# Attention steps in a fused attention and Hadamard-MLP kernel: order of bank emptying, place of the residual, and places of x transposes, values and folds

## The chip, the core and the metric

The kernel runs on one core of one Trainium2 chip. The metric is the time of the whole program on the device in microseconds (us); times given are medians of several runs, and beside them stands one profiled execution, from which all durations come. TensorE is called PE in the profile, VectorE DVE, ScalarE ACT, GpSimd POOL, SyncE SP. SP issues nearly all DMAs.

## What is computed

The input x has 8 batches of 512 rows with 512 features. One attention layer and one MLP layer follow each other, each with a layer norm ahead of it, a layer norm behind it and a residual sum:

```python
x = x + _layernorm(_L0_attn_ref(_layernorm(x, axis=-1), ...), axis=-1)
x = x + _layernorm(_L0_ffn_ref(_layernorm(x, axis=-1), ...), axis=-1)
```

The attention has 16 heads of 32 features. Its scores come from rotated queries and keys alone, since the rotary part is as wide as the head:

```python
c_kv = x @ W_dkv + b_dkv
v = (c_kv @ W_uv + b_uv).reshape(B_, S_, N_HEADS, D_HEAD)
c_q = x @ W_dq + b_dq
q_rot = apply_rotary((c_q @ W_qr + b_qr), cos, sin)
k_rot = apply_rotary((x @ W_kr + b_kr), cos, sin)
scores = einsum('bqhd,bkhd->bhqk', q, k) / sqrt(D_HEAD)
attn = softmax(scores)
out = einsum('bhqk,bkhd->bqhd', attn, v) @ W_o + b_o
```

The MLP is a gated one (512 to 2048 to 512) with Walsh-Hadamard transforms ahead of both matrix products. The second transform is folded into W_down: during the attention part, the kernel transforms W_down once, 32 of its 512 columns at a time (16 folds), and keeps the result in DRAM for the MLP.

## The kernel before

The program has two parts. The attention part runs to about 930 us, the MLP part behind it. The change lies in the attention part.

The attention of a batch is cut into 4 groups of 4 heads, and a group into 4 steps (one for each 128 keys). A batch so has 16 steps, called step 0 to step 15 here (`i` in the code; `c = i % 4` is the step in its group), and the part has 128 steps. The order of every instruction is written out by hand (`manual_schedule`); the engines work through their own queues in that order and wait for each other by semaphores.

In a step, PE gets these in turn:

- `scores_t` (lines 556 to 584): transposed scores `t` of 4 heads by 128 keys and 512 queries, in two score tiles of two banks each. Four bf16 matmuls (L564) put the negated row maximum in, eight matmul instructions (L573) add the scores. ACT takes the exponential of either tile (L584) into `p`.
- `weigh` (L602) of the step before: the product of `p` with the values, gathered in the bank `ops`. At the end of a group ACT copies it to `osb` (L611).
- in the third step of a group `sums` (L618), in the last `bias_rows`: four small transposes (L550) of the row maxima `parts`, which ACT copies to `brow` (L554) for the `t` of the next group.
- the piece of the table `BETWEEN`, unless the step is in `TWO`
- `row_max` (L527): the scores `s` of the step six ahead, whose row maxima DVE takes (two reduces, L535)
- the piece of `BETWEEN` in steps of `TWO`, this time in a score tile, and then the piece of the table `BEHIND`

Pieces are what the next batch (or the last one) needs: transposes of x (`x_flip`, L393, four transposes), the compressed queries and keys (`compress`, L406), keys and queries with their rotation (`key` L438, `query` L454, `rotate` L413), values (`value`, L466), the output projection of the batch before (`out_proj`, L656 and L657) and folds of W_down (`fold`, L485, with four levels on DVE, L493 and L494, one in each of the steps that follow, and a store by SP). With the rotation, ACT adds the bias, DVE shuffles (L419), and POOL makes two products and a sum (L420 to L422).

PSUM has three pools: `ps_s` with three score tiles of two banks, through which `t`, `s` and the pieces of `TWO` steps rotate, `ps_o` with one bank for `ops`, and `ps_f` with one bank, which all other pieces, the sums and the bias rows share. A piece can only start when the one before it has been copied out.

POOL gets the sums of neighbouring `p` (`add_up`, L590, four instructions in the second and in the fourth step of a group), the rotations, the inverse deviations (L104, L105), the residual sums (L689, in steps 10 to 13, by `early`), and the `split` of row maxima into three bf16 parts (L543 to L545, in the second step of a group). DVE has beside the reduces the sums of pairs (`add_pairs`, L595, first step of a group), statistics of rows, the division (L652) and the levels of the folds.

Of the kernel before, what the change touches and what calls it, by code (L numbers as in the profile page):

```python
# [10 lines left out]
F32 = mybir.dt.float32  # L11
# [22 lines left out]
def sandwich_kernel(  # L34
# [218 lines left out]
    with ExitStack() as actx:  # L253
# [127 lines left out]
        def x_norm(b, t):  # L381
            rs, sh = stats[b]
            xn[b, t] = row.tile([P, D], F32, tag="xn", name=f"xn_{b}_{t}", bufs=3)
            nc.scalar.activation(
                xn[b, t], xs[b][:, t, :], AF.Identity, bias=sh[:, t : t + 1], scale=rs[:, t : t + 1]
            )
# [130 lines left out]
        def row_max(n, qc):  # L517

            b, g = divmod(n, NK)
            if qc == 0:  # L520
                nms[n] = sm.tile([P, NT, GH], F32, tag="nm", name=f"nm_{n}")
            sp = [
                ps_s.tile([P, 2, S], F32, tag="s", name=f"s_{n}_{qc}_{h}") for h in range(2)
            ]
            for j in range(GH):
                rows = slice(j * DH, (j + 1) * DH)
                nc.tensor.matmul(  # L527
                    sp[j // 2][:, j % 2, :],
                    lhsT=qT[b][rows, g, ts(qc, P)],
                    rhs=kT[b][rows, g, :],  # L530
                    start=True,
                    stop=True,
                )
            for h in range(2):
                nc.vector.tensor_reduce(  # L535
                    nms[n][:, qc, 2 * h : 2 * h + 2], sp[h], AX.X, ALU.max, negate=True
                )
# [18 lines left out]
        def scores_t(n, c):  # L556

            b, g = divmod(n, NK)
            sp = [
                ps_s.tile([P, 2, S], F32, tag="s", name=f"t_{n}_{c}_{h}") for h in range(2)  # L560
            ]
            for j in range(GH):
                rows = slice(j * DH, (j + 1) * DH)
                nc.tensor.matmul(  # L564
                    sp[j // 2][:, j % 2, :],
                    lhsT=ones_b[rows, :],
                    rhs=brow[n][rows].rearrange("p t q -> p (t q)"),
                    start=True,
                    stop=False,
                )  # L570
            for j in range(GH):
                rows = slice(j * DH, (j + 1) * DH)
                nc.tensor.matmul(  # L573
                    sp[j // 2][:, j % 2, :],
                    lhsT=kT[b][rows, g, ts(c, P)],
                    rhs=qT[b][rows, g, :],
                    start=False,
                    stop=True,
                )
            for h in range(2):  # L580
                pt[n, c, h] = pp.tile(
                    [P, 2, S], F32, tag=f"p{c % 2}{h}", name=f"p_{n}_{c}_{h}", bufs=3 - c % 2
                )
                nc.scalar.activation(pt[n, c, h], sp[h], AF.Exp)  # L584

        def add_up(n, c):

# [9 lines left out]
        def weigh(n, c):  # L597
            b, g = divmod(n, NK)
            if c == 0:
                o_ps[n] = ps_o.tile([P, S], F32, tag="o", name=f"ops_{n}")  # L600
            for j in range(GH):
                nc.tensor.matmul(  # L602
                    o_ps[n][j * DH : (j + 1) * DH, :],
                    lhsT=vv[b][:, c, ds(g * P + j * DH, DH)],
                    rhs=pt[n, c, j // 2][:, j % 2, :],
                    start=(c == 0),
                    stop=(c == NT - 1),
                )
            if c == NT - 1:
                o_sb[n] = op.tile([P, S], F32, tag="osb", name=f"osb_{n}")  # L610
                nc.scalar.copy(o_sb[n], o_ps[n])  # L611

        def sums(n, parts=(2,)):

# [132 lines left out]
        row_max(0, 0)  # L747
        value(0, 0)
        row_max(0, 1)
        row_max(0, 2)  # L750
        key(0, 2)
        row_max(0, 3)
        query(0, 2)
        split(0)
        turn()
        for t in range(2):
            x_norm(1, t)
        x_flip(1, 0)
        row_max(1, 0)
# [3 lines left out]


        BETWEEN = {
            0: (x_flip, 1, 1), 1: (value, 0, 2), 4: (x_flip, 1, 2),
            8: (query, 1, 0), 9: (query, 1, 1), 12: (query, 1, 2),
        }
        BEHIND = {
            0: (value, 0, 1), 1: (key, 0, 3), 2: (query, 0, 3), 3: (value, 0, 3),  # L770
            4: (x_flip, 1, 3), 5: (compress, 1, "cq"), 6: (key, 1, 0), 7: (out_proj, -1, 0),
            8: (out_proj, -1, 1), 9: (out_proj, -1, 2), 10: (out_proj, -1, 3),
            11: (key, 1, 1), 12: (compress, 1, "ckv"), 13: (value, 1, 0), 14: (key, 1, 2),
            15: (x_flip, 2, 0),
        }
        OUT = {7: 0, 8: 1, 9: 2, 10: 3}

# [1 line left out]
        APART[NG - 2], APART[NG - 1] = (0, 2, 3), (0, 1, 2, 3)  # L779


        FOLDS = [3, 8, 13, 18, 24, 29] + [
            NK * NT * b + i for b in range(2, NB - 1) for i in (5, 13)
        ]
        READ = [0] + [g - 3 for g in FOLDS[1:]]

        TWO = (1, 5, 8, 9, 12)

        def piece(table, b, i, wide=False):
            if b == 0 and table is BEHIND and i == 8:  # L790
                out_bias()
            if i in table:
                fn, d, what = table[i]
                if 0 <= b + d < NB:
                    fn(b + d, what, *([True] if wide else []))
            if table is BETWEEN and NK * NT * b + i in FOLDS:
                fold(FOLDS.index(NK * NT * b + i), wide)
            if b == NB - 1 and (i, table is BEHIND) in ENTRY:
                in_step(*ENTRY[i, table is BEHIND], 2 * NT)
# [18 lines left out]
        def early(b, i):  # L818

            if b > 0 and i - 3 in OUT:  # L820
                residual(b - 1, OUT[i - 3])
            if b + 2 < NB:
                if i >= 14:
                    x_norm(b + 2, i - 14)
            if i < 2 and 0 < b + 1 < NB:
                x_norm(b + 1, i + 2)

        def later(b, i):

# [14 lines left out]
        for t in range(NG * NT):  # L844
            n, c = divmod(t, NT)
            b, i = divmod(t, NK * NT)
            if b == NB - 1 and i == NK * NT - AHEAD + 1:
                end.append(True)
            scores_t(n, c)
            turn()  # L850
            if c == 0 and n > 1:
                invert(n - 2)
            if c == 3 and n > 1:
                divide(n - 2)
            last_steps = t + AHEAD >= NG * NT
            if last_steps:
                piece(BETWEEN, b, i)
            if t > 0:
                weigh(*divmod(t - 1, NT))
            if c == 1 and n < NG - 1 or c == 3 and n < NG - 2:  # L860
                add_up(n, c)
            if n > NG - NK:
                if c == 1:
                    sums(n - 1, APART[n - 1])
            elif c == 2 and n > 0:
                sums(n - 1)
            if c == NT - 1 and n + 1 < NG:
                bias_rows(n + 1)
            if not last_steps and (i not in TWO or b == NB - 1):
                piece(BETWEEN, b, i)  # L870
            early(b, i)
            u = t + AHEAD
            if u < NG * NT:
                row_max(*divmod(u, NT))
                if u % NT == NT - 1:
                    split(u // NT)
            turn()
            if c == 0 and 0 < n <= NG - NK:
                add_pairs(n - 1)
            later(b, i)  # L880
            if b == 0 and i == 6:
                out_bias_in()
            if levels:
                levels.pop(0)()
            if small:
                small.pop(0)()
            if t in READ:
                fold_load(READ.index(t))
            if b == NB - 2 and i == 12:
                for j in range(3):  # L890
                    in_load(j)
            elif b == NB - 2 and i == 13:
                in_stats(0)
                in_stats(1)
            elif b == NB - 2 and i == 14:
                in_shift(0)
                in_shift(1)
            elif b == NB - 2 and i == 15:
                in_norm(0)
            elif b == NB - 1 and 2 <= i < 5:  # L900
                load_unit(*units[i - 2])
            elif b == NB - 1 and 12 <= i:
                load_row(b, i - 12)
            elif b == NB - 1 and i == 8:
                combine(*units[0][1:])
            if i in TWO and b < NB - 1:
                piece(BETWEEN, b, i, True)
            piece(BEHIND, b, i)
            if n == NG - 1 and c == 2:
                invert(NG - 2)  # L910

        weigh(NG - 1, NT - 1)
        b = NB - 1
        last = [
            ps_s.tile([P, 2, S], F32, tag="s", name=f"ps_y_{b}_{h}") for h in range(2)
# [560 lines left out]
```

## Time and profile before

| | us |
|---|---|
| median of 3 runs | 2175.89 (2175.66 to 2177.71) |
| the profiled execution | 2173.1 |
| its span, first to last instruction | 2171.3 |
| first `t` of batch 0 | 50.8 |
| first `t` of batches 1 to 7 | 155.5, 270.7, 382.1, 493.5, 604.9, 716.3, 826.5 |

The profile's page has the busy time of each engine, the chain that ended last and the costliest groups of instructions. A query for a stretch gives the same for that stretch: its busy columns stand in the order PE, PEld (weight loads), DVE, ACT, POOL, each with its count of instructions, then the granted clock of PE, the share of DMA and GB/s. The view of waits has a line for each waiting engine and line: who was waited for, us in total, times, longest. The timeline has start and length in us, engine, line, operation and tile (output<-input), and in brackets how long the engine stood idle ahead of it and who ended that. Busy times of PE include short waits, since the ends of matmuls are modelled.

### The profile page before, as it was taken

The page shows a single profiled execution, that of the slowest core. Times are in us where ns is not written, and L with a number is a line of the kernel's source. Part 1 is how long each engine was busy: PE and PEld are TensorE (multiplying, and loading weights), DVE is VectorE, ACT ScalarE, POOL GpSimd, SP SyncE. Part 2 cuts the span into 40 slices and gives each one's busy share as a digit, 9 for nine tenths or more (in the row PEclk, how much of TensorE's full clock was granted, in tenths as well). Part 3 has the DMA queues.
Part 4 walks back from the last instruction along what each step waited for, and adds up shares of the span by engine and source line. Part 5 has one row for each costly group of instructions (what it writes and reads, how often), then busy time and mean ns, then how long its engine had stood idle before and what let it go on. Part 6 is the DMA issues. An engine that isn't in the chain of part 4 may idle for free.

```text
span 2171.3 us, 24623 instructions
## 1 busy us (share of the span) xinstructions
PE 2115.1 (97%) x8552; PEld 971.1 (45%) x8552; DVE 1360.4 (63%) x2111; ACT 701.9 (32%) x1050; POOL 1352.1 (62%) x1433
## 2 busy tenths in 40 slices
PE   7999999999999999999999999999999999999998
PEld 3323333333333332334444465655556565555553
DVE  6686768686868676465655755657555557455432
ACT  3444555545454545522221121121122211111211
POOL 4686878787878879754554266464565644444542
PEclk9999999999999999999999999999999999999999
DMA  3112112111211122244344334242342333333321
GB/s 118 40 21 55 49 40 59 40 50 50 50 50 49 31 61 68 74 154 150 125 163 130 113 112 145 97 143 95 105 152 78 136 107 114 138 119 119 136 66 68
DMA packets 172252, 199.22 MB, mean 92 GB/s; under 512 B 85712, under 2 KB 114512, under 8 KB 172128
## 3 DMA queue, kind: packets, MB, share of 16 engines
q1 hardware_dynamic: 171776, 196.57, 28.7%
q8 instruction: 67, 1.10, 0.2%
q0 software_dynamic: 352, 1.08, 0.1%
q14 instruction: 57, 0.47, 0.1%
HBM read 154.24 MB, written 43.11 MB: 91 GB/s over the span
## 4 chain that ended last, share of the span: by engine, by line
PE 74%; DVE 10%; POOL 9%; issue 3%; DMA 2%; ACT 2%; POOLq 0%; SPq 0%; DVEq 0%; ACTq 0%
PE psy L1217 17%; PE d L1071 12%; PE g L1050 10%; PE u L1050 9%; POOL p L590 4%; PE s L527 3%; DVE nm L535 3%; PE ps_y L657 3%; PE t L573 3%; PE ops L602 3%; PE psz L1379 3%; PE ps_k L438 2%; PE ps_cq L406 1%; PE t L564 1%; DVE p L595 1%
## 5 line engine op out<-in xcount | busy, mean ns | idle before, releaser
L1217 PE MATMUL psy<-wd,g 128*128 128x512 f32 x896 | 436.9, 594 | 1.5 <-DVE g L1142 1.5
L535 DVE TENSOR_REDUCE nm<-s 128x2 f32<-128x1024 f32 x256 | 300.8, 1217 | 205.8 <-PE s L527 205.7
L590 POOL TENSOR_TENSOR p<-p,p 128x512 f32<-128x512 f32 x244 | 325.5, 1365 | 27.1 <-PE ops L602 19.4
L584 ACT ACTIVATE p<-t 128x1024 f32<-128x1024 f32 x256 | 248.2, 1021 | 104.1 <-PE t L573 104.1
L1091 POOL TENSOR_TENSOR h<-du,dm 128x256 f32<-128x256 f32 x92 | 66.8, 726 | 251.0 <-DVE du L1090 237.7
L1217 PEld LDWEIGHTS psy<-wd,g 128*128 128x128 f32 x896 | 169.8, 190 | 99.0 <-issue 82.5
L527 PE MATMUL s<-kT,qT 32*128 32x512 f32 x1024 | 156.7, 639 | 1.6 <-DVE nm L535 1.6
L1050 PE MATMUL u<-T,w_u 128*128 128x512 f32 x328 | 151.5, 592 | 2.8 <-DVE u3g L1169 2.8
L1050 PE MATMUL g<-T,w_g 128*128 128x512 f32 x328 | 151.3, 592 | 0.7 <-DVE T L248 0.7
L573 PE MATMUL t<-qT,kT 32*128 32x512 f32 x1024 | 142.9, 597 | 0.0
L602 PE MATMUL ops<-p,v 128*32 128x512 f32 x1024 | 136.8, 605 | 0.0
L1084 ACT COPY dm<-d 128x256 f32<-128x256 f32 x92 | 33.7, 366 | 299.0 <-PE d L1071 298.9
L438 PE MATMUL ps_k<-xT,wkr_sb 128*128 128x512 f32 x256 | 117.5, 601 | 0.8
L657 PE MATMUL ps_y<-wo_sb,oT 128*128 128x512 f32 x256 | 115.8, 593 | 0.6 <-DVE oT L652 0.6
L1050 PEld LDWEIGHTS g<-T,w_g 128*128 128x128 f32 x328 | 62.2, 190 | 78.6 <-issue 75.1
L1050 PEld LDWEIGHTS u<-T,w_u 128*128 128x128 f32 x328 | 61.8, 190 | 78.7 <-issue 73.2
L1071 PE MATMUL d<-tt,w 128*128 128x256 f32 x368 | 94.6, 380 | 0.4 <-DMA w<-w2d 0.3
L1050 PE MATMUL g<-xb,w_g 128*128 128x512 f32 x200 | 92.6, 592 | 1.2 <-issue 1.2
L1050 PE MATMUL u<-xb,w_u 128*128 128x512 f32 x200 | 92.5, 592 | 0.0
L1090 DVE TENSOR_TENSOR du<-d,du 128x256 f32<-128x256 f32 x92 | 39.1, 425 | 80.1 <-PE d L1071 76.6
L1071 PEld LDWEIGHTS d<-tt,w 128*128 128x128 f32 x368 | 69.6, 190 | 39.3 <-issue 27.0
L527 PEld LDWEIGHTS s<-kT,qT 32*128 32x128 f32 x1024 | 48.4, 183 | 78.0 <-issue 48.6
(242 smaller groups left out, 3781.0 us busy)
## 6 DMA issues: line engine op xcount, KB each, us to landing
wd<-wdd SPq DMA_DIRECT2D x112, 256.0 KB, 2.7
w_g<-wsd_g SPq DMA_DIRECT2D x24, 896.0 KB, 4.5
w_u<-wsd_u SPq DMA_DIRECT2D x23, 896.0 KB, 4.7
w<-w2d SPq DMA_DIRECT2D x23, 768.0 KB, 6.1
xr<-in_x SPq DMA_DIRECT2D x32, 256.0 KB, 2.9
xin<-x1d SPq DMA_DIRECT2D x32, 256.0 KB, 2.7
xres<-x1d SPq DMA_DIRECT2D x32, 256.0 KB, 3.2
out<-fy SPq DMA_DIRECT2D x32, 256.0 KB, 2.0
```

The costliest lines, as they stand in the source:

```text
L438: nc.tensor.matmul(ps, lhsT=wkr_sb[:, k, ts(g, P)], rhs=xT[b][:, k, :], start=(k == 0), stop=(k == NK - 1),)
L527: nc.tensor.matmul(sp[j // 2][:, j % 2, :], lhsT=qT[b][rows, g, ts(qc, P)], rhs=kT[b][rows, g, :], start=True, stop=True,)
L535: nc.vector.tensor_reduce(nms[n][:, qc, 2 * h : 2 * h + 2], sp[h], AX.X, ALU.max, negate=True)
L573: nc.tensor.matmul(sp[j // 2][:, j % 2, :], lhsT=kT[b][rows, g, ts(c, P)], rhs=qT[b][rows, g, :], start=False, stop=True,)
L584: nc.scalar.activation(pt[n, c, h], sp[h], AF.Exp)
L590: nc.gpsimd.tensor_add(into, into, pt[n, c, j // 2][:, j % 2, :])
L602: nc.tensor.matmul(o_ps[n][j * DH : (j + 1) * DH, :], lhsT=vv[b][:, c, ds(g * P + j * DH, DH)], rhs=pt[n, c, j // 2][:, j % 2, :], start=( ...
L657: nc.tensor.matmul(ps, lhsT=oT[b][:, k, ts(qc, P)], rhs=wo_sb[:, k, :], start=False, stop=(k == NK - 1),)
L1050: nc.tensor.matmul(ps, lhsT=w[:, SLOT[n], k, :], rhs=rhs[:, k, :], start=k == 0, stop=k == 1)
L1071: nc.tensor.matmul(ps, lhsT=lhs[m], rhs=rhs[m], start=True, stop=True)
L1091: nc.gpsimd.tensor_add(up[:, HS:], u3, m5)
L1217: nc.tensor.matmul(ys_[t], lhsT=g[:, ts(t, P)], rhs=w, start=n == 0, stop=n == NI - 1)
```

## The change

Six things are altered, and no operation is added or removed.

- The exponential of the second score tile: in the last step of a group it is issued behind `bias_rows`, and so behind the copy of `brow` on ACT. In the other steps it stays where it was.
- The copy of `ops` to `osb` gets a function of its own, `weighed`, which is called behind the piece of `BETWEEN`.
- `early` (the residual, the norm of x) is called behind `row_max` and `split`, no more ahead of them.
- Pieces change their steps: in `BETWEEN`, x transposes stand in steps 0, 1, 4 and 13; in `BEHIND`, values stand in steps 0, 3, 13 and 15, and steps 4 and 15 lose their x transposes. Value 1 of batch 0 is made ahead of the first step. The norms of x are issued in steps 12, 14, 15 and 0 in place of 14, 15, 0 and 1.
- Folds stand in steps 4 and 10 of batches 2 to 6 (before: 5 and 13), and at 4, 9, 14, 20, 26 and 31 of the first two batches (before: 3, 8, 13, 18, 24 and 29). In a step of `TWO` they take a score tile, in others they stand behind the piece of `BEHIND` and take the bank of the pieces.
- `TWO` is (8, 9, 10, 12, 14, 15), before (1, 5, 8, 9, 12).

```diff
--- before.py
+++ after.py
@@ -577,11 +577,15 @@
                     start=False,
                     stop=True,
                 )
-            for h in range(2):
+
+            def weight(h):
                 pt[n, c, h] = pp.tile(
                     [P, 2, S], F32, tag=f"p{c % 2}{h}", name=f"p_{n}_{c}_{h}", bufs=3 - c % 2
                 )
                 nc.scalar.activation(pt[n, c, h], sp[h], AF.Exp)
+
+            weight(0)
+            return lambda: weight(1)
 
         def add_up(n, c):
 
@@ -606,9 +610,10 @@
                     start=(c == 0),
                     stop=(c == NT - 1),
                 )
-            if c == NT - 1:
-                o_sb[n] = op.tile([P, S], F32, tag="osb", name=f"osb_{n}")
-                nc.scalar.copy(o_sb[n], o_ps[n])
+
+        def weighed(n):
+            o_sb[n] = op.tile([P, S], F32, tag="osb", name=f"osb_{n}")
+            nc.scalar.copy(o_sb[n], o_ps[n])
 
         def sums(n, parts=(2,)):
 
@@ -747,13 +752,14 @@
         row_max(0, 0)
         value(0, 0)
         row_max(0, 1)
+        value(0, 1)
         row_max(0, 2)
         key(0, 2)
         row_max(0, 3)
         query(0, 2)
         split(0)
         turn()
-        for t in range(2):
+        for t in range(3):
             x_norm(1, t)
         x_flip(1, 0)
         row_max(1, 0)
@@ -763,15 +769,15 @@
 
 
         BETWEEN = {
-            0: (x_flip, 1, 1), 1: (value, 0, 2), 4: (x_flip, 1, 2),
-            8: (query, 1, 0), 9: (query, 1, 1), 12: (query, 1, 2),
+            0: (x_flip, 1, 1), 1: (x_flip, 1, 2), 4: (x_flip, 1, 3),
+            8: (query, 1, 0), 9: (query, 1, 1), 12: (query, 1, 2), 13: (x_flip, 2, 0),
         }
         BEHIND = {
-            0: (value, 0, 1), 1: (key, 0, 3), 2: (query, 0, 3), 3: (value, 0, 3),
-            4: (x_flip, 1, 3), 5: (compress, 1, "cq"), 6: (key, 1, 0), 7: (out_proj, -1, 0),
+            0: (value, 0, 2), 1: (key, 0, 3), 2: (query, 0, 3), 3: (value, 0, 3),
+            5: (compress, 1, "cq"), 6: (key, 1, 0), 7: (out_proj, -1, 0),
             8: (out_proj, -1, 1), 9: (out_proj, -1, 2), 10: (out_proj, -1, 3),
             11: (key, 1, 1), 12: (compress, 1, "ckv"), 13: (value, 1, 0), 14: (key, 1, 2),
-            15: (x_flip, 2, 0),
+            15: (value, 1, 1),
         }
         OUT = {7: 0, 8: 1, 9: 2, 10: 3}
 
@@ -779,12 +785,13 @@
         APART[NG - 2], APART[NG - 1] = (0, 2, 3), (0, 1, 2, 3)
 
 
-        FOLDS = [3, 8, 13, 18, 24, 29] + [
-            NK * NT * b + i for b in range(2, NB - 1) for i in (5, 13)
+        FOLDS = [4, 9, 14, 20, 26, 31] + [
+            NK * NT * b + i for b in range(2, NB - 1) for i in (4, 10)
         ]
         READ = [0] + [g - 3 for g in FOLDS[1:]]
 
-        TWO = (1, 5, 8, 9, 12)
+
+        TWO = (8, 9, 10, 12, 14, 15)
 
         def piece(table, b, i, wide=False):
             if b == 0 and table is BEHIND and i == 8:
@@ -793,7 +800,7 @@
                 fn, d, what = table[i]
                 if 0 <= b + d < NB:
                     fn(b + d, what, *([True] if wide else []))
-            if table is BETWEEN and NK * NT * b + i in FOLDS:
+            if NK * NT * b + i in FOLDS and (table is BETWEEN) == (i in TWO):
                 fold(FOLDS.index(NK * NT * b + i), wide)
             if b == NB - 1 and (i, table is BEHIND) in ENTRY:
                 in_step(*ENTRY[i, table is BEHIND], 2 * NT)
@@ -819,11 +826,10 @@
 
             if b > 0 and i - 3 in OUT:
                 residual(b - 1, OUT[i - 3])
-            if b + 2 < NB:
-                if i >= 14:
-                    x_norm(b + 2, i - 14)
-            if i < 2 and 0 < b + 1 < NB:
-                x_norm(b + 1, i + 2)
+            if b + 2 < NB and i in (12, 14, 15):
+                x_norm(b + 2, max(i - 13, 0))
+            if i == 0 and 0 < b + 1 < NB:
+                x_norm(b + 1, 3)
 
         def later(b, i):
 
@@ -846,7 +852,10 @@
             b, i = divmod(t, NK * NT)
             if b == NB - 1 and i == NK * NT - AHEAD + 1:
                 end.append(True)
-            scores_t(n, c)
+            second = scores_t(n, c)
+            ends_group = c == NT - 1 and n + 1 < NG
+            if not ends_group:
+                second()
             turn()
             if c == 0 and n > 1:
                 invert(n - 2)
@@ -857,6 +866,9 @@
                 piece(BETWEEN, b, i)
             if t > 0:
                 weigh(*divmod(t - 1, NT))
+            if ends_group:
+                bias_rows(n + 1)
+                second()
             if c == 1 and n < NG - 1 or c == 3 and n < NG - 2:
                 add_up(n, c)
             if n > NG - NK:
@@ -864,23 +876,23 @@
                     sums(n - 1, APART[n - 1])
             elif c == 2 and n > 0:
                 sums(n - 1)
-            if c == NT - 1 and n + 1 < NG:
-                bias_rows(n + 1)
             if not last_steps and (i not in TWO or b == NB - 1):
                 piece(BETWEEN, b, i)
-            early(b, i)
+            if c == 0 and n > 0:
+                weighed(n - 1)
             u = t + AHEAD
             if u < NG * NT:
                 row_max(*divmod(u, NT))
                 if u % NT == NT - 1:
                     split(u // NT)
+            early(b, i)
             turn()
             if c == 0 and 0 < n <= NG - NK:
                 add_pairs(n - 1)
             later(b, i)
             if b == 0 and i == 6:
                 out_bias_in()
-            if levels:
+            if levels and i > 0:
                 levels.pop(0)()
             if small:
                 small.pop(0)()
@@ -910,6 +922,7 @@
                 invert(NG - 2)
 
         weigh(NG - 1, NT - 1)
+        weighed(NG - 1)
         b = NB - 1
         last = [
             ps_s.tile([P, 2, S], F32, tag="s", name=f"ps_y_{b}_{h}") for h in range(2)
```

## The prediction

> **What bounds the kernel now.** I read the totals of the page, then the waits of TensorE in the attention part alone, then its order of time at the places where those waits lie.
>
> ```profile
> span 2171.3 us, 24623 instructions
> PE 2115.1 (97%) x8552; PEld 971.1 (45%) x8552; DVE 1360.4 (63%) x2111; ACT 701.9 (32%) x1050; POOL 1352.1 (62%) x1433
> 493.50:604.90 111.40, 109.08 (x617) 37.58 (x616) 83.04 (x102) 57.82 (x76) 89.74 (x91) 1.00 0.19 49
> ```
>
> The third line is a busy table over one batch (steps of batch 4): TensorE 109.1 of 111.4 us, POOL 89.7, DVE 83.0. TensorE is the bound, and the diff neither adds nor removes a matmul of it. The listed waits of TensorE between 60 and 930 us add to 21 us only:
>
> ```profile
> PE t L564 <- DVE nm L535: 9.7, 16, 1.5
> PE ps_b L550 <- POOL parts L545: 4.3, 6, 0.9
> PE ps_v L466 <- ACT xT L396: 1.4, 6, 0.2
> PE ps_y L656 <- ACT brow L554: 1.2, 6, 0.2
> ```
>
> But ends of matmuls are modelled, so short waits hide in "busy". I therefore took from the timeline the time from the start of one group of matmuls to the start of the next, and subtracted the shortest such spacing of the same pair of groups in all 128 steps. Per step 0 to 15, mean of batches 2 to 5, in us: 1.10, .27, .49, .48, .48, .48, .11, .27, .18, .27, .01, .29, .29, 0, .43, .90: 6.05 a batch. Batches 0 and 1 lose 10.2 and 7.7, batch 6 5.5, batch 7 7.9. So 55 us in all can be had at most, 2.5%.
>
> Two kinds of wait make nearly all of it. First the score banks: `t` and `s` rotate through three double banks, so the second half of the next `t` needs the first row maximum of this step. The s group begins at T, its first reduce ends at T + 2.45 (493.05 + 1.2 against s at 491.87 below), TensorE needs 1.07 for s and then d for what stands behind it. The wait is 1.38 - d: .78 behind an x transpose (d = .6), .32 behind a value (1.06), .42 behind a fold (.96), none behind a 3.6 us projection. Second the one bank of the pieces, which ACT must empty. The step border 15 to 0 shows both, with POOL's queue ahead of it:
>
> ```profile
> 488.11 1.45 POOL L689 TENSOR_TENSOR y<-xr,y 128x512 f32<-128x512 f32 x1
> 491.24 0.25 POOL L545 CAST parts<-nm 128x16 bf16<-128x16 f32 x1
> 491.54 0.40 PE L550 MATMUL ps_b<-ident_b,parts 128*128 128x128 bf16 x4 [0.83 <-POOL parts L545]
> 491.87 1.14 PE L527 MATMUL s<-kT,qT 32*128 32x512 f32 x8
> 492.94 0.66 PE L393 MATMUL xt<-ident,xn 128*128 128x128 f32 x4
> 493.05 2.35 DVE L535 TENSOR_REDUCE nm<-s 128x2 f32<-128x1024 f32 x2 [1.97 <-PE s L527]
> 493.53 0.39 PE L564 MATMUL t<-brow,ones_b 32*128 32x512 bf16 x2
> 494.32 0.39 PE L564 MATMUL t<-brow,ones_b 32*128 32x512 bf16 x2 [0.41 <-DVE nm L535]
> ```
>
> The reader sees the residual's 1.45 us ahead of the split, .83 us of TensorE waiting for the split, then .79 between the halves of `t`.
>
> **What the Trainium skill says.** "PSUM — Partial Sum Buffer", Specifications: 8 banks of 512 fp32; the pools here take 6 + 1 + 1, so no bank is spare, and the waits above agree. "TensorE: Matmul & The Clock Gate", Architectural detail: ScalarE and VectorE are strict FIFO, so a late instruction delays all behind it; the trace agrees (starts keep program order). "SBUF — State Buffer", Who interferes with whom: DVE and GpSimd share a port pair as an exclusive lock; a DVE tensor_tensor with two SBUF inputs contends, tensor_reduce never. The trace agrees: half a fold level takes .42 us with POOL idle and 1.44 beside it, while a reduce stays at 1.2:
>
> ```profile
> 426.65 0.41 DVE L493 TENSOR_TENSOR fa<-fz 128x256 f32<-128x256 f32 x1
> 426.99 0.42 DVE L494 TENSOR_TENSOR fa<-fz 128x256 f32<-128x256 f32 x1
> 481.73 1.44 DVE L493 TENSOR_TENSOR fa<-fz 128x256 f32<-128x256 f32 x1
> 483.09 1.49 DVE L494 TENSOR_TENSOR fa<-fz 128x256 f32<-128x256 f32 x1
> ```
>
> **The change part by part**, for a batch of 2 to 5.
>
> *Second exponential behind brow (last step of a group).* brow's copy starts after its transposes (516.09 in step 3 of batch 4) instead of after the second exponential (516.6), so .45 earlier. The waits of `ps_y` (.27, step 7) and `ps_k` (.19, step 11) go: -.45; a 3.6 us piece follows, so no bank wait takes their place. In step 3 the value's .16 goes, but `t` then waits to .32 in all: 0. The exponential itself ends about 1 us later, 517.7, and frees its bank .4 us before the next `t`: free. If that cover went, it would cost up to .3 a group.
>
> *Residual behind the split.* Only in step 13 do both fall together. POOL's five small casts come 1.27 to 1.45 earlier: the .90 of step 15 goes. The residual's own reader, a store two steps later, isn't near.
>
> *`osb` copied behind the transposed x.* The value's .31 in step 0 goes, but its `t` then meets the bank wait .32: 0.
>
> *Pieces moved.* Step 15 gets a value for an x transpose: bank wait .79 to .32, -.47. Step 1 has a transpose ahead of s for a value in a score bank: its .25 wait for the exponential goes, one more change of tile shape costs .09. Step 2's .49 came from the wide bank and a level on DVE in steps 0 and 1; both are gone. Steps 3 to 5: the fold stands behind s in step 4 in place of a transpose, -.37. Step 13 keeps .32. x_norm (.82 on ACT) moves from steps 0, 1, 14, 15 to 12, 14, 15, 0: ACT is 52% busy, its slack in step 12 is over 1 us: 0. SP: the fold's load and store move one to six steps, each has three steps of slack; loads of x wait for x_norm one step earlier: 0.
>
> Sum so far -.45 -.90 -.47 -.25 +.09 -.49 -.37 = -2.84.
>
> *The second fold, step 13 to step 10.* Its four levels move from steps 13, 14, 15, 0 to 11, 12, 13, 14, the only part that can cost. On DVE the level of step 12 stands ahead of the shuffle of q and of the reduces of step 13. Today:
>
> ```profile
> 476.63 1.23 DVE L111 SCALAR_TENSOR_TENSOR sh_y<-mvy,rs_y 128x1 f32<-128x1 f32 x1
> 477.79 0.73 DVE L419 STREAM_SHUFFLE rot_q<-lin_q 128x512 f32<-128x512 f32 x1
> 477.80 1.27 POOL L689 TENSOR_TENSOR y<-xr,y 128x512 f32<-128x512 f32 x1
> 479.45 2.36 DVE L535 TENSOR_REDUCE nm<-s 128x2 f32<-128x1024 f32 x2 [0.93 <-PE s L527]
> ```
>
> There is .93 us of slack. I moved this queue on by hand. Step 10 is longer by .96 (fold), step 11 shorter by .19, so TensorE's `t` of step 13 stands at 475.8. The level in step 11 runs beside POOL's sums (L590, 1.22 each) and ends at 471.7; k's shuffle, rc and the reduces of step 12 end at 475.05 (today 472.8), the pair sums, alternating with POOL, at 478.5, the shift at 479.85. POOL then has nothing but q's rotation, which needs the shuffle: it is idle, so the level of step 12 takes its short .8, and the first reduce runs 481.3 to 482.5. s has been ready since 479.85. `t` of step 14 could start at 480.8 (step 13 is .4 shorter without the fold) and waits until 482.55: 1.75 in place of .32, **+1.43**. POOL ends the sums of step 13 at 490.7, the split at 492.7; its transposes are due at 493.4: no wait in step 15. Bounds: 0 if the level of step 11 finds gaps in POOL's sums; +4.3 if both levels take 2.9 (wait 3.7) and the split is late again by .9.
>
> Net -1.4 a batch, batches 2 to 6: -7.0.
>
> *Batch 1*: its step 1 loses 1.59, to a fold level on DVE: .32 after; with the same items as above, +.4 for a fold in a score bank of step 15 that waits for the delayed exponential, and +1.43: -2.3. *Batch 0*: value 1 goes among the first row maxima, where TensorE waits for DVE (16 matmuls from 32.63 to 38.29): its 1.06 is hidden, -1.06, or 0 if not; a fold fills step 9's bank wait (-.7) and the .58 of step 15 goes, while levels cost some .4: -2.0 in all. *Batch 7*: behind step 15 of batch 6 now stands a value, where nothing stood: 1.85 to .32: -1.6 with the rest.
>
> Sum -7.0 - 2.3 - 2.0 - 1.6 = **-12.9 us**. The profiled execution took 2173.1 (span 2171.3), so 2160.2; the median, 2175.9, lies 2.8 above it: **2163.0**.
>
> **Rivals.** (1) *No crowding on DVE*: the level of step 11 slips into gaps; then 1.43 x 7 = 10 us more are won, **2153**. For it: levels of .42 exist; against: POOL runs without a gap from 457 to 500. (2) *Waits are only handed on*: the split is late again because POOL is behind, and brow's .45 turns up elsewhere: 1.35 x 7 = 9.5 back, **2172**. For it: two of my items already end so. (3) *Slower*: in steps 11 to 13 DVE and POOL lock each other out twice, the reduce of step 13 comes 2 us later than I say, and the late POOL delays the split by .9: 2.9 x 7 = +20, **2183**. It decides from a wait of 3.6 us in step 14 on. For it: batch 0, which has levels in steps 11 and 12 today, shows .94 in step 14 without any of the output projection's work; against: POOL stands still while it waits for the shuffle, which shortens the level.
>
> **How the numbers follow.** Forecast .50 (own range 2157 to 2170), rival 1 .20, rival 2 .17, rival 3 .13. A measurement tells about .2% from no change, 4.4 us: 2171.5 to 2180.2 is "same". Forecast, rival 1 and a third of rival 2 are faster: .75; the rest of rival 2 same: .12; rival 3 slower: .13. Range 2152 to 2174: all but rival 3 and the tails.
>
> **What would show it.** After: no wait of ps_b for parts; xT and brow gone from TensorE's waits; step 15's half-wait of .79 down to .32; the reduce of step 13 directly behind q's shuffle and 1.2 to 1.8 us between the halves of `t` in step 14; POOL idle before q's rotation. Past 920 us nothing may move. Wrong if step 14 shows .3 or over 3 us, or if the split still ends last in step 15.

## The result, and the profile after

The changed kernel takes 2161.6 us (median of 4 runs, 2160.6 to 2162.6) against 2176.3 before (4 runs): a ratio of 0.9932, 95% interval 0.9914 to 0.9949. The profiled execution took 2160.6 us, with a span of 2158.8. So 14.7 us are won by the medians, 12.5 by the spans; the forecast was 12.9.

From the first `t` of batch 0 to the last of batch 7 the profiled executions differ by 9.9 us.

The list of the change leaves out one alteration that the diff shows: no fold level is taken in step 0 any more (`levels and i > 0`). For the folds of batches 2 to 6 it does nothing, because with their new places no level would come due there. It acts on two folds of the first two batches.

These lines are of the page and of the busy table of batch 4 of the changed kernel (columns as before).

```profile
span 2158.8 us, 24605 instructions
PE 2111.5 (98%) x8552; PEld 969.0 (45%) x8552; DVE 1348.7 (62%) x2111; ACT 703.1 (33%) x1050; POOL 1353.6 (63%) x1433
487.53:597.13 109.60, 108.81 (x618) 37.17 (x618) 79.94 (x102) 57.80 (x77) 90.17 (x91) 1.00 0.20 49
```

The batch takes 109.6 in place of 111.4 with the same matmuls. DVE's busy time fell by 3 us although it does the same: the 16 instructions of the fold levels took 13.6 us in place of 17.5, the pair sums 12.8 in place of 11.3, and the reduces of the row maxima the same to .1. The waits of TensorE in the attention part are now these, among others.

```profile
PE t L564 <- DVE nm L535: 12.2, 14, 1.9
PE ps_b L550 <- POOL parts L545: 0.9, 1, 0.9
PE ps_b L550 <- ACT p L585: 0.8, 5, 0.2
```

The waits for `parts` fell from 4.3 to 0.9 (one, in batch 0), those for `xT` and for `brow` behind a group's border are no longer there, and the wait for the row maximum has grown from 9.7 to 12.2 in fewer places. The last line is what is left in step 15 of batches 1 to 5. The border of steps 15 and 0 (batches 3 and 4), where before `t` waited .79 and `ps_b` .83:

```profile
484.42 0.59 POOL L545 CAST parts<-nm 128x16 bf16<-128x16 f32 x1
484.91 1.26 POOL L694 TENSOR_TENSOR y<-xr,y 128x512 f32<-128x512 f32 x1
485.07 0.40 PE L550 MATMUL ps_b<-ident_b,parts 128*128 128x128 bf16 x4 [0.17 <-ACT p L585]
485.40 1.14 PE L527 MATMUL s<-kT,qT 32*128 32x512 f32 x8
486.47 1.12 PE L466 MATMUL ps_v<-wuv_sb,ckv 128*128 128x512 f32 x2
487.53 0.71 PE L564 MATMUL t<-brow,ones_b 32*128 32x512 bf16 x4
487.86 0.81 PE L573 MATMUL t<-qT,kT 32*128 32x512 f32 x4
```

The residual (L694) now stands behind the last cast, the transposes follow the cast within .06 us, and the four matmuls of `t` are one row again: between 487.53 and 487.86 lies a wait of .10, and its second part (.22) comes behind the row at 487.86, .32 in all. The value behind `s` fills what the x transpose did not.

Ahead of the transposes the view names ACT's exponential, which ended at 485.04, .03 behind the last cast. It isn't what they wait for: in the kernel of the second experiment below they start .2 us before that exponential ends. So the split still ends last in step 15, and .24 us of waiting are left.

The two traces were then laid side by side by the start of each step's first `t`. Change per step, changed kernel less before, in us, batches 3 to 5 (equal to .02 in all three): step 0 -.78, 1 -.22, 2 -.49, 3 -.16, 4 +.31, 5 -1.01, 7 -.25, 10 +.95, 11 -.19, 13 -.47, 14 +.68, 15 -.19; sum -1.81. Some of these are work that changed its step (a fold from 5 to 4, from 13 to 10; .46 more work in step 15). By batch, 0 to 6: -.9, -2.5, 0, -1.8, -1.8, -1.8, -2.1; batch 7 up to its last `t` +.9. The rest is .9 ahead of the first `t` (step 0 of batch 0 is .93 longer in return, which its -.9 contains) and 1.7 behind the last `t`, in the MLP part, which took 1252 to 1255 us in the executions of all kernels here, however their attention part looked.

The crowding on DVE, ahead of step 14; the first three lines are the level of step 11 and the pair sums of step 12:

```profile
461.85 1.50 DVE L493 TENSOR_TENSOR fa<-fz 128x256 f32<-128x256 f32 x1
463.28 1.48 DVE L494 TENSOR_TENSOR fa<-fz 128x256 f32<-128x256 f32 x1
467.66 3.63 DVE L599 TENSOR_TENSOR p<-p,p 128x1024 f32<-128x1024 f32 x2
471.22 1.22 DVE L111 SCALAR_TENSOR_TENSOR sh_y<-mvy,rs_y 128x1 f32<-128x1 f32 x1
471.79 1.14 PE L527 MATMUL s<-kT,qT 32*128 32x512 f32 x8
472.36 0.41 DVE L493 TENSOR_TENSOR fz<-fa 128x256 f32<-128x256 f32 x1
472.70 0.41 DVE L494 TENSOR_TENSOR fz<-fa 128x256 f32<-128x256 f32 x1
473.05 0.72 DVE L419 STREAM_SHUFFLE rot_q<-lin_q 128x512 f32<-128x512 f32 x1
473.66 2.33 DVE L535 TENSOR_REDUCE nm<-s 128x2 f32<-128x1024 f32 x2
473.84 1.27 POOL L420 TENSOR_TENSOR lin_q<-lin_q,cs 128x512 f32<-128x512 f32 x1 [1.42 <-DVE rot_q L419]
473.92 0.39 PE L564 MATMUL t<-brow,ones_b 32*128 32x512 bf16 x2
474.92 0.39 PE L564 MATMUL t<-brow,ones_b 32*128 32x512 bf16 x2 [0.61 <-DVE nm L535]
```

`s` starts at 471.79, so its maximum could be taken from 472.97 on; DVE comes to it at 473.66, behind the level of step 12 and the shuffle, and POOL stands idle for 1.42 us meanwhile. 1.00 us lies between the halves of `t`: less the .22 that they need, and with the .22 behind it, a wait of 1.01.

### The profile page after: what moved, and what is told of

Read it like the earlier page. It is cut to its first block, busy times and chain, and to the rows that moved or that the text cites. A ratio compares the mean times of both kernels' runs of the same rounds, so it can differ in the third digit from the quotient of the medians.

```text
span 2158.8 us, 24605 instructions
## 1 busy us (share of the span) xinstructions
PE 2111.5 (98%) x8552; PEld 969.0 (45%) x8552; DVE 1348.7 (62%) x2111; ACT 703.1 (33%) x1050; POOL 1353.6 (63%) x1433
## 4 chain that ended last, share of the span: by engine, by line
PE 86%; DVE 9%; POOL 2%; issue 1%; ACT 1%; DMA 0%; SPq 0%; POOLq 0%; DVEq 0%; ACTq 0%
PE psy L1230 17%; PE d L1084 13%; PE u L1063 10%; PE g L1063 10%; PE s L527 5%; PE ps_y L662 5%; PE ops L606 5%; PE ps_k L438 4%; PE t L573 4%; PE psz L1392 3%; DVE nm L535 2%; PE t L564 2%; PE l L623 1%; DVE p L599 1%; PE ps_cq L406 1%; PE fxh L223 1%
## 5 line engine op out<-in xcount | busy, mean ns | idle before, releaser
L599 DVE TENSOR_TENSOR p<-p,p 128x1024 f32<-128x1024 f32 x56 | 86.1, 1577 | 0.0
```

The lines of the kernel that those rows point to most:

```text
L599: nc.vector.tensor_add(into, into, pt[n, 0, h])
```

## Experiments

All were measured beside the kernel before, whose median was 2177.1 to 2177.4 in them. An edit is against the changed kernel, if nothing else is said. Since runs of one kernel differ by up to 8 us, the verdicts rest on the steps of the profiled executions. In batches 3 to 6 these agree to some .02 us where nothing was changed. Single steps of the other batches don't: step 1 of batch 1 differs by 1.60 and step 6 of batch 2 by 1.65 us between kernels that are the same there.

**Is it the levels that make step 14 wait?**

```diff
-            if levels and i > 0:
+            if levels and (i > 0 or b > 2) and not (b > 1 and i in (11, 12)):
```

> The changed kernel, but the levels of the fold of step 10 (batches 2 to 6) wait until steps 13, 14, 15 and 0, where they stood before the change; the fold itself stays in step 10. Theory (VectorE's queue: the level of step 12 stands ahead of the shuffle of q and of the reduces of step 13): the wait in step 14 falls from 1.01 to 0.32 and the 0.24 of step 15 goes, 0.93 us in each of batches 2 to 5, so about 3.7 us in all: 2158. Rival A (the wait of step 14 comes from the transpose and its bank in step 13, not from the levels): no change, 2161.6, step 14 stays at 1.0. Rival B (the level in step 0 brings back step 2's wait of 0.49, as in the kernel before): 2 us of it are lost again, 2160.

Measured 2165.5 us (ratio 0.9955, 0.9941 to 0.9968), slower than the changed kernel. Step 14 fell to .32 in batches 2 to 5, and the .24 of step 15 went in batches 3 to 5, as the theory has it; rival A is out. But step 2 lost 1.9, 2.0 or 3.5 us in batches 3 to 6 (the level stands in step 0 ahead of it), not .49: rival B is right in kind and much too small in size. In the kernel before, a value and a key stood behind `s` in step 1, now only the key. That this lost cover makes the difference in size was not tested.

**The level in step 1 instead of 0**

```diff
-            if levels and i > 0:
+            if levels and i > 0 and not (b > 1 and i in (11, 12)):
```

> The changed kernel; in batches 2 to 6 the levels of the fold of step 10 wait until steps 13, 14, 15 and 1 (not 0, where the pair sums stand). Theory (what came back in step 2 with late levels was the level in step 0, behind the pair sums and ahead of the reduces of step 1): step 2 stays at 0, step 14 at 0.32 and step 15 at 0, in batches 2 to 5: -3.7 us against the changed kernel, 2158. Rival (a level anywhere in steps 0 to 2 costs it, since step 1 has only the key behind its reduces): step 2 or 3 gains 1 to 3 us of waiting, 2162 to 2170.

Measured 2158.2 us (0.9913, 0.9900 to 0.9927). Batches 3 to 5 take 108.67 us in place of 109.60: step 14 at .32, step 15 at 0, step 2 at 0, as expected. This settles the +1.43 of the forecast's queue as mechanism; its size was .69, and .24 in step 15. Step 0 of batch 7 became 2.5 us shorter as well, and step 5 of batch 7 2.7 longer.

**The three orders, undone one at a time**

```diff
+            early(b, i)
             u = t + AHEAD
...
-            early(b, i)
             turn()
```

> The changed kernel, with the residual and the norm of x ahead of row_max and split again. Theory (POOL's queue is what the bias rows of step 15 wait for; today they start 0.06 us after the parts are done): the residual's 1.27 to 1.45 us on POOL come on top in step 15 of batches 1 to 5, and about half of it in batch 6: +7 us, 2169. Rival (the gain of this edit was handed on, POOL has slack): +0 to +1.5 us, at most 2163.

Measured 2167.8 us (0.9965, 0.9951 to 0.9979). Step 15 is longer by 1.33 to 1.34 in each of batches 1 to 5, .87 in batch 6; 2.2 of it come back in step 0 of batch 7. POOL's queue is the one that the bias rows wait for.

```diff
             ends_group = c == NT - 1 and n + 1 < NG
-            if not ends_group:
-                second()
+            second()
...
             if ends_group:
                 bias_rows(n + 1)
-                second()
```

> The changed kernel, with both exponentials ahead of the copy of brow in the last step of a group. Theory: the bank waits 0.27 in step 7 and 0.19 in step 11 come back in all but the first batches, 0.45 a batch, and the value in step 15 waits as in step 3, which its next bank wait absorbs: +3 us, 2164.6. Rival (brow also gates the value of step 15 and the t of the next group by its full 0.45 to 1 us, 32 groups): +10 us or more, 2172.

Measured 2163.9 us (0.9944, 0.9930 to 0.9959). +.25 in step 7 and +.19 in step 11, in batches 1 to 6; +.16 in step 3 and -.16 in step 4: the forecast's three items to .02. But step 14 became .20 to .25 shorter in batches 1 to 4, which the forecast did not have: most likely the .19 of step 11 gives the queue on DVE that much more time. Batches 3 and 4 so lose .2 each, not .44. The rival is out.

```diff
                 weigh(*divmod(t - 1, NT))
+                if c == 0:
+                    weighed(n - 1)
...
-            if c == 0 and n > 0:
-                weighed(n - 1)
```

> The changed kernel, with the copy of ops to osb behind the product again, so ahead of the copy of the transposed x on ScalarE. Theory: the value of step 0 waits 0.31 for its bank and the t behind it waits 0.31 less for the row maximum; the same in step 4 with the fold: 0, 2161.6. Rival (the wait of the value is not absorbed): 0.31 in step 0 and in step 4 of 7 batches, +4 us, 2166.

Measured 2164.7 us (0.9950, 0.9936 to 0.9963). The last `t` is at 908.2 us against 906.7, of which .65 was there at the second step of batch 0. Steps 0 and 1: +.31 and -.31; steps 4 and 5: +.31 and -.21. The wait is handed on, but for .10 a batch. By its median this kernel is 3.0 us slower than the changed one, nearer to the rival's 2166. But of the 3.4 us between the profiled executions 2.0 lie behind the last `t` (1254.1 against 1252.1), where the edit changes nothing, and the steps speak for the theory.

**Orders alone, places alone.** The first is the kernel before with the three orders; the second the changed kernel with all three edits above.

> The kernel before, with the three orders alone (second exponential behind brow, residual behind split, osb behind the transposed x), all pieces, folds and norms in their old places. Theory (each order removes one wait of the kernel before): step 15 loses its 0.9, step 7 0.25, step 11 0.19, while the 0.31 of step 0 and the 0.16 of step 3 turn up one step later; 1.35 a batch in batches 2 to 5, about 1 in batches 0, 1 and 6 together with less in 7: -7.5 us against the kernel before, 2169. Rival (the orders only pay with the new places): -2 us at most, 2174.

Measured 2183.7 us (1.0030, 1.0021 to 1.0040): **slower than before**. Steps 15, 7 and 11 won their .88, .25 and .19, but steps 1 and 2 lost 1.7 and .6 to 2.3 in batches 3 to 6. Neither theory nor rival had that. DVE and POOL in steps 0 and 1 of batch 4, and TensorE's wait:

```profile
504.91 4.39 DVE L599 TENSOR_TENSOR p<-p,p 128x1024 f32<-128x1024 f32 x2
509.22 1.48 DVE L493 TENSOR_TENSOR fw<-fa 128x256 f32<-128x256 f32 x1
510.63 1.48 DVE L494 TENSOR_TENSOR fw<-fa 128x256 f32<-128x256 f32 x1
512.03 2.34 DVE L535 TENSOR_REDUCE nm<-s 128x2 f32<-128x1024 f32 x2
506.29 6.94 POOL L594 TENSOR_TENSOR p<-p,p 128x512 f32<-128x512 f32 x4 [0.28 <-PE ops L606]
513.29 0.39 PE L564 MATMUL t<-brow,ones_b 32*128 32x512 bf16 x2 [1.42 <-DVE nm L535]
514.43 0.39 PE L564 MATMUL t<-brow,ones_b 32*128 32x512 bf16 x2 [0.74 <-DVE nm L535]
```

In the kernel before, the same pair sum took 2.35 us, since POOL happened to stand still from 500.5 to 502.0:

```profile
500.53 2.35 DVE L595 TENSOR_TENSOR p<-p,p 128x1024 f32<-128x1024 f32 x2
502.00 6.04 POOL L590 TENSOR_TENSOR p<-p,p 128x512 f32<-128x512 f32 x4 [1.50 <-ACT p L584]
```

With step 15 shortened, step 0 begins sooner, but POOL has the residual behind the split now: its sums of the group before begin 2.76 us behind the first `t` of step 0, in place of 1.65. Its pause shrinks from 1.50 to .28, the two adders meet, and the pair sum takes 4.39. The level behind it pushes the maximum of step 1 to 512.0, though `s` (506.1) was ready at 507.3.

> The changed kernel with all three orders undone, so the new places alone. Theory (the parts add up): the 1.34 of step 15 in batches 1 to 5 and 0.87 in batch 6, the 0.25 and 0.19 of steps 7 and 11, and the 0.31 that only moves: +10 to +11 us against the changed kernel, 2172, so 4 to 5 us faster than before. Rival (orders and places overlap, e.g. the late split hides behind the wait of step 14): +5 us, 2167.

Measured 2168.6 us (0.9962, 0.9949 to 0.9974), nearer to the rival in us. By steps the theory is right in batches 3 to 5 (+1.63 each: 1.33 in step 15, .25 in step 7, .19 in step 11, .10 in steps 3 to 5, and -.24 in step 14 as above), but batch 7 gives 2.8 back. So the places alone win 8.5 us, the orders alone lose 6.6, and both together win 14.7, each against the median of the kernel before that was measured beside it.

**Is it the level in step 0?** The orders alone, with that level in step 1:

```diff
-            if levels:
+            if levels and i > 0:
                 levels.pop(0)()
```

> The kernel before with the three orders alone, and no fold level in step 0 (the level that stood there goes to step 1). Theory (the orders alone lost 6.6 us because POOL and the pair sums of step 0 now meet, and the level in step 0 stands behind these and ahead of the reduces of step 1): the added waits of steps 1 and 2 go, 1.7 and 0.6 to 2.3 us in batches 2 to 6, and the old 0.49 of step 2 with them: -13 us against the orders alone, 2170, so 7 us faster than before. Rival (the loss comes from osb or the second exponential being late, not from the level): steps 1 and 2 stay as they were with the orders alone, 2182 to 2184.

Measured 2170.4 us (0.9975, 0.9964 to 0.9985). Step 1's loss fell from 1.70 to .21, step 2 shows -.49 against before in batches 2 to 6. One condition, 13 us, as expected; the rival is out.

**Batch 2 and batch 7**

The next edit stands on top of the levels in steps 13, 14, 15 and 1; it takes the last fold of the early ones a step earlier, and two of its levels at once in step 15.

```diff
-        FOLDS = [4, 9, 14, 20, 26, 31] + [
+        FOLDS = [4, 9, 14, 20, 26, 30] + [
...
                 levels.pop(0)()
+                if t == 31:
+                    levels.pop(0)()
```

> The kernel with the levels in steps 13, 14, 15 and 1, and the last fold of batch 1 in step 14 in place of 15, its first level in step 15, so that its last level leaves step 4 of batch 2. Theory (that level, behind the pair sums of step 4, makes the 2.03 of step 6 of batch 2): step 6 of batch 2 falls to 0, step 15 of batch 1 from 0.7 to 0.3 or less: -2.4 us, 2155.8. Rival (the wait of batch 2 comes from the first load of a group or from the sums on POOL alone): no change, 2158.

Measured 2156.1 us (0.9903, 0.9890 to 0.9917), the fastest here, faster than both kernels. The 2.03 of step 6 of batch 2 is gone, and all of batches 2 to 5 take 108.67 or 108.68. The cause was the same as in step 0: a level behind the pair sums of a group's first step. It stood in step 4 because none may be taken in step 0. In the changed kernel:

```profile
295.83 4.09 DVE L599 TENSOR_TENSOR p<-p,p 128x1024 f32<-128x1024 f32 x2
299.84 1.48 DVE L493 TENSOR_TENSOR fw<-fa 128x256 f32<-128x256 f32 x1
301.24 1.48 DVE L494 TENSOR_TENSOR fw<-fa 128x256 f32<-128x256 f32 x1
302.65 2.34 DVE L535 TENSOR_REDUCE nm<-s 128x2 f32<-128x1024 f32 x2
```

Two edits of batch 6 aimed at step 0 of batch 7. The first, on top of the levels in steps 13, 14, 15 and 1:

```diff
-            elif b == NB - 2 and i == 14:
+            elif b == NB - 2 and i == 15:
                 in_shift(0)
                 in_shift(1)
-            elif b == NB - 2 and i == 15:
                 in_norm(0)
```

> As the kernel with the levels in steps 13, 14, 15 and 1, and in batch 6 the two shifts of the rows for the MLP's entry (in_shift, L111, which wait on VectorE for POOL) go from step 14 to step 15, behind its reduces. Theory (the 3.35 of step 0 of batch 7 comes from these two standing ahead of the reduces of step 15): it falls to 0.3 to 1.0, the transposes of step 0 may wait up to 1 for their rows: -2.5 us more, 2155.5. Rival (POOL's backlog sets it through k's rotation): step 0 of batch 7 stays over 2, no gain.

Measured 2162.2 us (0.9929, 0.9917 to 0.9942), 4 us slower than without it. The wait between the halves of `t` in step 0 of batch 7 did fall, from 1.28 to .32, so the shifts were what stood in the way; but the transposes of the rows for the MLP then waited 3.28 us for their norm, which came behind the reduces, a level and the shifts on DVE. So step 0 of batch 7 is 3.7 us longer than without the edit, of which step 5 gives .9 back. 1.6 of the 4 us lie elsewhere, in step 6 of batch 2 (3.68 in place of 2.03), which the edit doesn't touch.

> As the kernel with the last fold of batch 1 in step 14, and in batch 6 the rows for the MLP's entry are loaded in step 9 and their statistics taken in step 12 (before: 12 and 13), so that POOL makes their inverse deviations ahead of the sums and the split of step 13. Theory (VectorE's shifts wait for these in step 14, ahead of the reduces of step 15): step 0 of batch 7 falls from 1.3 to 0.3 or 0.5. What is won there is lost again in step 5 of batch 7 where POOL waits for weights of the MLP that come by DMA: 0 to -1 us, 2155 to 2156. Rival (step 5 doesn't depend on it): -1 us and step 5 unchanged.

Here the loads of the rows stand in step 9 and the statistics in step 12, on top of the fold in step 14. Measured 2158.2 us (0.9914, 0.9900 to 0.9927), no faster than without. The wait between the halves of `t` in step 0 of batch 7 fell from 1.30 to .32, as the theory had it, but the value there then waited .77 for DVE to empty its bank, so the step won only .21, and steps 14 and 15 of batch 6 lost .60. The gain in time failed to come. What is fixed behind it shows in POOL's own waits, 835 to 846 us, in the kernel with the levels in steps 13, 14, 15 and 1:

```profile
POOL w_u L146 <- DMA w_u<-in_w_upT: 2.6, 1, 2.6
```

The changed kernel waits .8 there. POOL combines weights of the MLP in step 4 of batch 7 and waits for their load; that kernel wins 2.5 us in step 0 of batch 7 and loses 2.7 in step 5. That the load's landing bounds this stretch would fit, but no run moved the load, so it stays open.

## Why the prediction was right, point by point

- *Second exponential behind brow, -.45*: .25 and .19, and the .16 of step 3 handed on to step 4. Right for these waits; but in the changed kernel the .19 of step 11 comes back as .20 to .25 more waiting in step 14, which the sum left out.
- *Residual behind the split, -.90*: undone, it costs 1.34, nearly the whole of the residual; what was won is .90 less the .24 that was left. The forecast had 0 left, and had named a split that still ends last in step 15 as a sign of being wrong. This part was wrong by that .24.
- *osb behind xT, 0*: +.31 and -.31. Right; in steps 4 and 5 it is worth .10, which the forecast left out.
- *Value in step 15, -.47*: wait .79 to .32. Right. The rule 1.38 - d gave .32 for steps 0, 1, 3, 4 and 5; all show .32 (step 5 was put at .42).
- *Step 2, -.49*: right, but put down to the wide bank and the levels together. The runs show that it is the level in step 0, and that it would have grown to 2 to 4 us once step 15 became shorter. The forecast summed the orders as if each stood alone; alone they lose. The sum came out because the places took that level away: in the changed kernel the pair sums of step 0 take 4.1 us too (494.06 to 498.19), but the reduces follow them directly.
- *Levels in steps 11 to 14, +1.43*: same mechanism and order on all three engines, the idle POOL (1.42 us) and the short level (.82) included. The size was off: +.69. The level of step 11 took 2.9 beside POOL and the pair sums of step 12 took 3.63 (3.45 forecast), but the chain as a whole came .84 sooner against `t` of step 12 than I had it: the level of step 11 ended .16 earlier, the reduces of step 12 .52, the shuffle .73. In the listing ahead of step 14 a row on DVE starts some .06 to .1 us before the row ahead of it ends (472.36 and .41 against 472.70; 473.05 and .72 against 473.66); I had added about nine such rows end to end, which would make most of the .84. So the reduce stood .69 behind the readiness of `s` (473.66 against 472.97) in place of 1.45.
- *Batches*: 0 to 6 were put at -.9 (with value 1 counted where it shows, in batch 7), -2.3, then five times -1.4; measured -.9, -2.5, 0, -1.8, -1.8, -1.8, -2.1. Batch 2 was missed: the last fold of batch 1 leaves a level in its step 4, 2.03 us. Batch 1 came out by luck: the 1.59 of its step 1 was to fall to .32 and is 2.00 in the changed kernel, with a level ahead of the reduces still, while step 2 gained 2.49, more than it was put at.
- *Batch 7, -1.6 and -1.06 for its missing value*: +.9. This is the step that failed. I took its 1.85 of step 0 for a bank wait that a value would fill. By my own rule a bank wait is at most 1.38 long. The kernel before already shows what else it was (`s` in step 15 of batch 6):

```profile
825.19 1.14 PE L527 MATMUL s<-kT,qT 32*128 32x512 f32 x8
825.79 0.16 DVE L111 SCALAR_TENSOR_TENSOR sh_f<-mvf,rs_f 128x1 f32<-128x1 f32 x1 [0.63 <-POOL rs_f L105]
827.09 2.34 DVE L535 TENSOR_REDUCE nm<-s 128x2 f32<-128x1024 f32 x2
```

The reduce could have begun at 826.37, and began .72 later: two shifts on DVE stood ahead of it and waited for POOL. So a value could have covered 1.06 of the 1.85 at best (an estimate from these lines). In the changed kernel they come later still:

```profile
814.53 0.16 DVE L111 SCALAR_TENSOR_TENSOR sh_f<-mvf,rs_f 128x1 f32<-128x1 f32 x1 [0.63 <-POOL rs_f L105]
815.83 2.35 DVE L535 TENSOR_REDUCE nm<-s 128x2 f32<-128x1024 f32 x2
817.10 0.39 PE L564 MATMUL t<-brow,ones_b 32*128 32x512 bf16 x2 [1.90 <-DVE nm L535]
```

Here `s` began at 812.68, and its maximum comes 1.97 us late. The experiments show both parts of it: with the levels of batch 6 moved away, step 0 of batch 7 is 2.5 us shorter, and with the shifts moved, the rest of this wait goes to .32.

From the first to the last `t`, then, 9.9 us were won of 12.9. Batches 3 to 5 won .4 us more each than forecast and batch 6 .7, batches 2 and 7 fell short by 1.4 and 3.6, and .9 us ahead of the first `t` and 1.7 us of the MLP part, which the change doesn't touch, made up for most of that. The total was as near as it was partly by luck; the mechanisms of the middle batches were not luck.

- *What would show it*: the waits for `xT` and `brow` are gone, step 15's half-wait is .32, the reduce stands directly behind the shuffle, and POOL is idle ahead of q's rotation, as forecast. But the halves of `t` in step 14 lie 1.00 apart where 1.2 to 1.8 was said, one wait for `parts` is left (.9, in batch 0), and the MLP part moved by 1.7.
- *Rival 1* is out: the halves of the level of step 11 took 1.50 and 1.48 beside POOL. (Its 10 us counted the 1.43 seven times; the forecast charges it in six batches, 8.6 us.) *Rival 2* is out as a whole, since the gains stand by step; in part it is right, for osb and for the .19 of step 11. *Rival 3* didn't occur in the changed kernel, but its mechanism, two adders that lock each other out, is what made the orders alone slower than before.

The Trainium skill, "SBUF — State Buffer", Who interferes with whom, carried most of this: a DVE sum with two SBUF inputs and a GpSimd instruction that reads SBUF exclude each other. The traces agree: a pair sum of two instructions took 2.35 us where POOL stood still when it began, and 4.39 beside it; the reduces from PSUM took 1.2 in both.

## What to carry to other kernels

Where a tensor engine is 98% busy, wins lie in short waits: take the spacing of instruction groups against its minimum, and for each ask what is late next. For a bank rotation, write down how much work must stand behind a product until its reader is through (here 1.38 us beyond `s`), and fill it with pieces of about that length. A removed wait brings the next work sooner: look at what that work meets on the other engines, above all DVE sums beside GpSimd sums, and take work that can wait (here levels of a fold) out of the queue between such a sum and a reader that the tensor engine waits for.

## What the runs showed that I had not expected

- Three orders that each remove a wait made the kernel 0.3% slower together, and one level of 3 us in another step turned this into 0.25% faster.
- A gap of 1.5 us in POOL's queue, which no list of TensorE's waits shows, was worth 2 us of pair sum (2.35 against 4.39).
- A change of tile shape costs TensorE .09 to .10 us (from the last start of a group of 128x128 tiles to the start of the next group it is .52 where that has another tile shape and .43 where it has the same; two matmuls of a value ahead of a key .43, ahead of `t` .52); the prediction's .09 for step 1 fits its -.22 only roughly, and the cost was not tested by itself.
- The MLP part differed by up to 3.7 us between executions of kernels in which it is the same.
